# Four graph layers on one core: transposes by VectorE and transfers in place of TensorE, and a planner with other costs

## The chip, the cores and the metric

The kernel runs on one core of a Trainium2 chip. The core has a matrix engine (TensorE, PE in the profile), three engines that work on tiles (VectorE or DVE, ScalarE or ACT, GpSimd or POOL), an engine that issues transfers (SyncE or SP), and 16 DMA engines. The metric is the device time of one execution in microseconds (us), as the median of several runs.

## The reference, cut to what matters

32 graphs, each with 512 nodes of 256 features and its own 512x512 matrix `adj`, go through four layers. Each layer adds a graph network's output to its input and normalizes the rows. All is in 32-bit floats.

```
x = ln(x + relu(((1 + eps)*x + adj @ x) @ W1 + b1) @ W2 + b2)        # layer 0, hidden width 512
x = ln(x + prelu(adj @ (x @ W.T + b)))                               # layer 1
h = ln(x)*gamma + beta                                               # layer 2
x = ln(x + x + relu((adj @ h) @ W_rel + b_rel + h @ W_root))
g = (eps*x + adj @ x) @ W1 + b1                                      # layer 3, hidden width 1024
x = ln(x + silu(g * rsqrt(mean(g*g) + 1e-6) * w) @ W2 + b2)
```

## The kernel before, in words

Each graph is one batch of work. An activation `x` lies in a tile of 128 partitions by 4x256: node `4p + c` is in partition `p`, chunk `c`. All the large products are built as two-by-two block products with seven multiplications in place of eight (`seven`, with block sums made by VectorE in `left_sums` and `right_sums`). `aggregate` makes `adj @ x` in transposed form, features on partitions; `dense_feat` makes the hidden layers with features on partitions; `dense_add` goes back to nodes on partitions and adds onto `x`.

Layer 2 also needs `h` itself with features on partitions. In `layer2` TensorE makes it: 8 transposes of 128x128 (`flip`) into PSUM per batch, then two copies of 128x512. Layer 3 needs the rms scale of each node in every partition, since nodes lie along the columns there: `column_sums` sums over partitions, `inv_sqrt` takes the power on GpSimd, and 4 transposes spread the 512 scales over a PSUM bank `pr`, which VectorE's multiplications then read.

The `1 + eps` of layer 0 and the `eps` of layer 3 are added to the diagonal blocks of `adj` and of two of its block sums (`with_loops`). The four plain blocks are kept in a tile (`kept`, by tile-to-tile transfers, `carry`) and carried back after layer 0 (`restore`). The row vectors `b2` of layers 0 and 3 are added by GpSimd (`plus_row`, four additions of 128x256 each).

The order of all instructions is written out by a planner when the program is built. `Plan.add` records each operation with its possible engines, its cost and its readers and writers. `Plan.order` then places one operation at a time on the engine where it can end first, by a rank that grows with the batch number (`period`) and with the need of TensorE (`needs`); up to `FLIGHT` batches are under way at once. Tiles come from pools (`rooms` of 128x1024, `smalls`, PSUM `banks`), of which a part is held in reserve (`spare`) for older batches. Several rules (`RULES`) are tried, and the one whose plan ends first is taken. The engines then execute the written order, each its own queue in order, and wait on semaphores where operations depend on each other. Transfers are all on SyncE's queue. The planner's costs are fixed numbers: for a transfer, `ISSUE` on the queue, `ADVANCE` until data move, a time by size, and `AFTER` until the reader may start. While `Plan.order` holds a `port` as taken, an operation of VectorE that reads and writes SBUF and one of GpSimd do not overlap.

Of the kernel before, what the change touches and what calls it, by code (L numbers as in the profile page):

```python
# [14 lines left out]
P = 128  # L15
# [11 lines left out]


def in_psum(x):
    return isinstance(x, Part) and x.room.pool.psum  # L30
# [35 lines left out]
def gpsimd_time(n):  # L66
    return 0.15 + n * 0.0024, 0.05


def power_time(n):  # L70
    return 0.37 + n * 0.158, 0.04
# [4 lines left out]
ISSUE, ADVANCE, AFTER, LANES = 0.45, 1.5, 0.35, 8  # L76
# [6 lines left out]
HAND = dict(tensor=0.25, vector=0.13, scalar=0.13, gpsimd=0.18, sync=0.2)  # L83

# [10 lines left out]
RULES = [(50, 2, last, near) for last in (12, 20) for near in (0, 0.5, 1)]  # L95


class Pool:

# [5 lines left out]
    def clear(self):  # L105
        self.rooms = [None] * len(self.tiles)

    def free(self):

        return sorted(  # L110
            (0.0 if r is None else r.until, i)
            for i, r in enumerate(self.rooms)
            if r is None or not r.left
        )


class Room:


    def __init__(self, pool):  # L120
        self.pool = pool
        self.uses = 0
        self.clear()

    def clear(self):
        self.index = None
        self.left = self.uses
        self.until = 0.0


class Part:
# [34 lines left out]
    def place(self):  # L166
        v = self.room.pool.tiles[self.room.index]
        for step in self.steps:
            v = step(v)
        return v  # L170
# [3 lines left out]
class Op:  # L174
# [4 lines left out]
    rank: tuple  # L179
    ways: dict  # L180
    port: set
    yields: bool
    kbytes: float
    rooms: list = field(default_factory=list)
# [6 lines left out]
class Plan:  # L191
# [10 lines left out]
    def grains(self, x):  # L202
        part = isinstance(x, Part)
# [4 lines left out]
        for step, n in dims[:-1]:  # L208
            starts = [s + step * i for s in starts for i in range(n)] if step else starts
        step, n = dims[-1]  # L210
        return {
            (key, g)
            for s in starts
            for g in range(s // grain, (s + step * (n - 1)) // grain + 1)
        }

    def add(self, ways, out, ins, ordered=None, port=(), kbytes=0):
        me = len(self.ops)
        op = Op(self.graph, (self.graph, me), ways, port, "scalar" in ways, kbytes)
        self.ops.append(op)  # L220
        before, results = set(), set()
        writes = self.grains(out) if out is not None else set()
# [22 lines left out]
    def do(self, out, *ways, ordered=None, scrap=None):  # L245
# [3 lines left out]
        port = set()  # L249
        for e, method, _, args, kw in ways:  # L250
            tiles = [x for x in (*args, *kw.values()) if isinstance(x, (bass.AP, Part))]
            ins += tiles
            if e == "gpsimd" and kw.get("op") != ALU.pow or e == "vector" and not (
                method.startswith("bn_") or any(in_psum(x) for x in tiles)
            ):
                port.add(e)
# [19 lines left out]
    def move(self, out, src, kbytes, inward=True):  # L276


        def issue():
            self.nc.sync.dma_start(*(x.place() if isinstance(x, Part) else x for x in (out, src)))  # L280

        self.add(
            {"sync": ((ISSUE, ADVANCE + wire_time(kbytes) + AFTER), issue)},
            out if inward else None, [src] if isinstance(src, Part) else [], kbytes=kbytes,
        )
# [31 lines left out]
    def order(self, period, pace, last, near):  # L317
# [15 lines left out]
        oldest, port, wire, lanes = 0, 0.0, 0.0, [0.0] * LANES  # L333
        can_start = {i for i, n in enumerate(behind) if not n}
        done = []
        while can_start:
# [4 lines left out]
            def rooms_free(op):  # L341

                count = {}
                for r in op.rooms:
                    if r.index is None:
                        count[r.pool] = count.get(r.pool, 0) + 1
                at = 0.0
                for pool, n in count.items():
                    if pool not in room_at:
                        room_at[pool] = pool.free()  # L350
                    n += pool.spare[min(op.graph - oldest, len(pool.spare) - 1)]
                    if op.graph - oldest >= self.flight or n > len(room_at[pool]):
                        return None
                    at = max(at, room_at[pool][n - 1][0])
                return at

            best = {}
            for i in can_start:
# [4 lines left out]
                if op.kbytes:  # L363
                    wait = max(wait, lanes[0])
                at = {
                    e: max(free[e], wait, ready[i][e], port if e in op.port else 0.0)
                    for e in op.ways
                }
                way = min(at, key=lambda e: at[e] + sum(op.ways[e][0]) + (YIELD if op.yields and e == "vector" else 0.0))
# [10 lines left out]
            end = t + busy + tail  # L380
            if op.kbytes:
                wire = max(wire, t + ADVANCE) + wire_time(op.kbytes)
                end = wire + AFTER
                lanes = [*lanes[1:], end]
            if engine in op.port:
                port = end
            for r in op.rooms:
                if r.index is None:
                    r.index = r.pool.free()[0][1]
                    r.pool.rooms[r.index] = r  # L390
# [16 lines left out]
def tile_gnn_stack(ctx: ExitStack, tc: tile.TileContext, a: dict, out: bass.AP):  # L407
# [36 lines left out]
    FLIGHT, ROOMS, SMALL = 4, 36, 12  # L444
# [3 lines left out]
    psum = ctx.enter_context(tc.tile_pool(name="psum", bufs=1, space=bass.MemoryType.PSUM))  # L448
    plan = Plan(nc, FLIGHT)

# [7 lines left out]
    rooms = pool(work, "room", ROOMS, NC * D, P, (0, 4, 6, 8))  # L458
# [5 lines left out]

    def gpsimd(method, n, *args, **kw):
        return "gpsimd", method, gpsimd_time(n), args, kw
# [22 lines left out]
    def both(method, o, x, y, engines):  # L489
        plan.do(o, *(e(method, span(o), x, y) for e in engines))  # L490

    def add(o, x, y, *engines):
        both("tensor_add", o, x, y, engines or (vector,))

    def sub(o, x, y, *engines):
        both("tensor_sub", o, x, y, engines or (vector,))

    def mul(o, x, y):
        both("tensor_mul", o, x, y, (vector,))
# [10 lines left out]
    def carry(o, x):  # L510
        plan.move(o, x, P * span(o) / 256)

    def inv_sqrt(o, x):
        n = span(o)
        plan.do(
            o, ("gpsimd", "tensor_tensor", power_time(n), (x, mhalf[:, 0:n]), dict(op=ALU.pow))
# [3 lines left out]
    def room(*shape):  # L520
        return Part(Room(rooms)).shaped(*shape)

# [57 lines left out]
    nc.vector.memset(mhalf, -0.5)  # L580

# [52 lines left out]
    class Adjacency:  # L634
# [3 lines left out]
        def __init__(self, b):  # L638

            self.halves = [room(HC, N) for _ in range(2)]  # L640
            for m in range(NC):
                chunk = self.halves[m // HC][:, m % HC, :]
                plan.move(chunk, a["adj"][b][:, m, :], P * N / 256)
# [6 lines left out]
        def sums(self):  # L650
# [8 lines left out]
            kept = room(4, HC, P)  # L659
            self.plain = [kept[:, i] for i in range(4)]  # L660
            for d, o in zip(self.plain, self.loops):
                if plan.graph:
                    carry(d, o)
                else:
                    copy(d, o)

        def restore(self):
            for d, o in zip(self.plain, self.loops):
                carry(o, d)

        def with_loops(self, loop):
            for d, o in zip(self.plain, self.loops):
                add(o, d, loop.unsqueeze(1).to_broadcast(list(o.shape)), vector)

        def row_sums(self):

            rows = room(N)
# [79 lines left out]
    def dense_sums(upper, lower):  # L757
# [3 lines left out]
        for pairs in zip(upper, lower):  # L761
            blocks = [x[:, :, j * TH : (j + 1) * TH] for x in pairs for j in range(2)]
            sums = right_sums(*blocks, [room(2, TH) for _ in range(3)], blocks[1])
# [29 lines left out]
    def column_sums(t, put):  # L793
# [3 lines left out]
        few = small(16)  # L797
# [7 lines left out]
        for q in range(1, P // Q):  # L805
            add(few[0:Q], few[0:Q], few[q * Q : (q + 1) * Q])
        for q in range(P // Q):
            put(slice(q * Q, (q + 1) * Q), few[0:Q, q :: P // Q])
# [64 lines left out]

    def plus_row(x, r):

        for c in range(NC):
            add(x[:, c, :], x[:, c, :], r, gpsimd)
# [13 lines left out]
    def load_x(b):  # L891
        x = tok()
        plan.move(x, a["x"][b].rearrange("(p c) d -> p c d", c=NC), N * D / 256)
# [192 lines left out]
```

## Time and profile before

| | before |
|---|---|
| median of 3 runs | 2365.41 us (2363.45 to 2366.38) |
| profiled execution, own time | 2366.02 us |
| its span, first to last instruction | 2364.2 us |
| TensorE busy | 2330.0 us, 14362 matrix instructions |
| VectorE busy | 2138.4 us, 5485 instructions |
| ScalarE busy | 1570.1 us |
| GpSimd busy | 407.7 us |
| granted TensorE clock | 0.997 |
| bytes moved by transfers | 107.25 MB, 45 GB/s on average |

Every 32-bit matrix product appears as two matrix instructions in the profile, a transpose as one. Nearly all instructions carry the same line number, that of the function in which the planner issues them, so groups are told apart by the names of their tiles: `ps` is PSUM, `room` a work tile, `few` a small tile, `L_gnn_W` and `A` weights and sums of weights, `ident` the identity matrix that a transpose uses. The length of an instruction includes the pipeline's depth, so that two neighbours overlap; what one costs in a full queue is the distance between starts.

### The profile page before, as it was taken

How to read it: one execution, taken by the hardware profiler on the slowest of the kernel's cores; microseconds unless marked ns; L12 is line 12 of the kernel's file. 1: busy time of each engine (PE TensorE's matmuls, PEld its weight loads, DVE VectorE, ACT ScalarE, POOL GpSimd, SP SyncE). 2: the span in 40 equal slices, each digit the busy share in tenths (PEclk: the TensorE clock that was granted, in tenths of full speed). 3: DMA queues.
4: the chain of work that ended last, by engine and by line, in shares of the span. 5: the costliest groups of instructions: out<-in, count | busy, mean ns of one | idle time of the engine just before them, and what ended most of it. 6: DMA issues, size and time to landing. Idle time of an engine off the chain costs nothing.

```text
span 2364.2 us, 40948 instructions
## 1 busy us (share of the span) xinstructions
PE 2330.0 (99%) x14362; PEld 2135.4 (90%) x14362; DVE 2138.4 (90%) x5485; ACT 1570.1 (66%) x3994; POOL 407.7 (17%) x422
## 2 busy tenths in 40 slices
PE   8999999999999999999999999999999999989997
PEld 7899989999999999999999999999999989978997
DVE  6899989999999999999999999999999999988997
ACT  3767666667666676766676666776666766565764
POOL 1112111111121121111111211111111112111111
PEclk9999999999999999999999999999999999999999
DMA  7001110111110111101111101111011111011000
GB/s 218 12 8 54 50 54 12 52 50 51 53 35 30 50 54 50 54 14 50 50 52 52 44 20 50 54 50 54 14 50 50 52 52 46 23 52 48 10 10 28
DMA packets 103487, 107.25 MB, mean 45 GB/s; under 512 B 10865, under 2 KB 78193, under 8 KB 103281
## 3 DMA queue, kind: packets, MB, share of 16 engines
q1 hardware_dynamic: 103280, 104.64, 14.5%
q8 instruction: 113, 1.85, 0.3%
q14 instruction: 94, 0.76, 0.1%
HBM read 54.80 MB, written 16.78 MB: 30 GB/s over the span
## 4 chain that ended last, share of the span: by engine, by line
PE 91%; DVE 4%; DMA 2%; ACT 1%; issue 1%; SPq 0%; POOL 0%; POOLq 0%; ACTq 0%; DVEq 0%
PE ps L266 91%; DVE room L266 3%; ACT room L266 1%; DVE few L266 1%; DMA room<-in_x_dram 1%; ACT scrap L266 1%; DMA room<-room 1%; SPq L280 0%; DMA L_gnn_eps<-in_L_gnn_eps_dram 0%; DMA room<-in_adj_dram 0%; POOL few L266 0%; ACT L266 0%; POOLq L1082 0%; DVE L_gnn_W L266 0%; DVE A L266 0%
## 5 line engine op out<-in xcount | busy, mean ns | idle before, releaser
L266 PE MATMUL ps<-room,room 128*128 128x256 f32 x3584 | 911.9, 380 | 9.8 <-DMA room<-in_x_dram 5.8
L266 DVE TENSOR_TENSOR room<-ps,room 128x256 f32<-128x256 f32 (+1 forms) x1344 | 629.6, 475 | 149.3 <-PE ps L266 122.6
L266 PEld LDWEIGHTS ps<-room,room 128*128 128x128 f32 x3584 | 650.1, 191 | 88.8 <-issue 7.1
L266 DVE TENSOR_TENSOR room<-room,room 128x512 f32<-128x512 f32 (+1 forms) x1120 | 640.6, 585 | 9.9 <-ACT room L266 3.1
L266 PE MATMUL ps<-L_gnn_W,room 128*128 128x128 f32 (+1 forms) x3584 | 622.7, 291 | 7.2 <-ACT room L266 4.9
L266 PEld LDWEIGHTS ps<-L_gnn_W,room 128*128 128x128 f32 x3584 | 525.3, 192 | 31.1 <-ACT room L266 7.2
L266 PE MATMUL ps<-A,room 128*128 128x128 f32 x3072 | 489.2, 276 | 1.8 <-ACT room L266 1.1
L266 PEld LDWEIGHTS ps<-A,room 128*128 128x128 f32 x3072 | 434.8, 192 | 15.8 <-ACT room L266 1.3
L266 PE MATMUL ps<-room,L_gnn_W 128*128 128x256 f32 x1536 | 424.6, 380 | 1.0 <-DVE room L266 0.9
L266 ACT ACTIVATE room<-ps,L_gnn_b_c 128x256 f32<-128x256 f32 x768 | 318.2, 472 | 157.2 <-PE ps L266 157.0
L266 POOL TENSOR_TENSOR few<-few,mhalf 128x4 f32<-128x4 f32 (+1 forms) x160 | 212.5, 1329 | 1211.0 <-DVE few L266 1208.5
L266 ACT ACTIVATE room<-ps 128x256 f32<-128x256 f32 (+1 forms) x546 | 215.0, 407 | 298.5 <-PE ps L266 294.7
L266 ACT ACTIVATE room<-room,few 128x256 f32<-128x256 f32 x624 | 341.0, 603 | 107.0 <-DVE few L266 103.7
L266 DVE TENSOR_TENSOR room<-room 128x256 f32<-128x256 f32 (+1 forms) x640 | 330.4, 518 | 18.0 <-DMA room<-in_adj_dram 5.7
L266 POOL TENSOR_TENSOR room<-room,L_gnn_b 128x256 f32<-128x256 f32 x256 | 194.6, 769 | 739.6 <-PE ps L266 519.0
L266 PE MATMUL ps<-room,A 128*128 128x256 f32 x1152 | 319.2, 380 | 3.0 <-ACT room L266 3.0
L266 PEld LDWEIGHTS ps<-room,L_gnn_W 128*128 128x128 f32 x1536 | 279.7, 191 | 33.1 <-DVE room L266 2.2
L266 ACT ACTIVATE room<-room 128x1024 f32<-128x1024 f32 (+2 forms) x260 | 245.8, 946 | 18.1 <-DVE room L266 16.5
L266 ACT ACTIVATE room<-room,L_gnn_rms_weight_c 128x512 f32<-128x512 f32 x256 | 179.7, 718 | 111.3 <-DVE room L266 108.2
L266 PEld LDWEIGHTS ps<-room,A 128*128 128x128 f32 x1152 | 206.5, 191 | 27.1 <-ACT room L266 4.2
L266 ACT ACTIVATE scrap<-room 128x256 f32<-128x256 f32 x384 | 157.2, 411 | 74.3 <-DVE room L266 63.1
L266 ACT ACTIVATE scrap<-room,few 128x256 f32<-128x256 f32 x384 | 190.7, 498 | 18.1 <-DVE few L266 16.3
(53 smaller groups left out, 1453.4 us busy)
## 6 DMA issues: line engine op xcount, KB each, us to landing
room<-in_adj_dram SPq DMA_DIRECT2D x128, 256.0 KB, 5.0
room<-room SPq DMA_DIRECT2D x252, 128.0 KB, 2.2
room<-in_x_dram SPq DMA_DIRECT2D x32, 512.0 KB, 6.0
out_dram<-room SPq DMA_DIRECT2D x32, 512.0 KB, 3.0
L_gnn_W<-in_L_gnn_W_dram SPq DMA_DIRECT2D x2, 1024.0 KB, 8.5
L_gnn_W<-in_L_gnn_W_dram SPq DMA_DIRECT2D x2, 512.0 KB, 8.1
L_gnn_b<-in_L_gnn_b_dram SPq DMA_DIRECT2D x3, 128.0 KB, 5.0
L_gnn_W_rel<-in_L_gnn_W_rel_dram SPq DMA_DIRECT2D x1, 256.0 KB, 7.2
```

Of the source, the lines that this page charges most:

```text
L266: getattr(getattr(self.nc, engine), method)(to, *(put(x) for x in args), **kw)
```

## The change

- **Transposes of h** (`turned`). For all but the first and last batch (`alone`), VectorE transposes 32x32 squares of `h` in two instructions of 128x512, and 16 tile-to-tile transfers of 32 KB carry the squares to their partitions.
- **Scales of layer 3** (`everywhere`). For the same batches, VectorE arranges the scales in a 32x32 square and transposes it; one transfer writes 16x32 numbers to a line in DRAM, a second reads the line into all 128 partitions. The multiplications read this tile where they read PSUM.
- **Diagonals.** From the second batch on, the two blocks of `adj` itself are read again from the input (four transfers of 64 KB), the two of the block sums are stored in DRAM and read back. `with_loops` works in place.
- **Row additions** (`plus_row`) go from GpSimd to VectorE, as two additions of 128x512.
- **Planner.** A tile-to-tile transfer has an issue time of its own, `AFTER` is longer, some loads have an additional `late`, the power costs more, and the power on GpSimd takes part in the port's rule. Dependencies are kept by 32 partitions as well. Tiles can be given out as halves (`short`). Batches in flight are 5 where they were 4, `smalls` 11 where they were 12, the reserves are smaller, and there are three rules with other numbers.

```diff
-ISSUE, ADVANCE, AFTER, LANES = 0.45, 1.5, 0.35, 8
+ISSUE, ADVANCE, AFTER, LANES = dict(sync=0.45, within=0.66, gpsimd=1.5), 1.5, 0.8, 8
...
+TWO_OPERANDS = ("tensor_add", "tensor_sub", "tensor_mul", "scalar_tensor_tensor")
+PORT = 0.25
...
-RULES = [(50, 2, last, near) for last in (12, 20) for near in (0, 0.5, 1)]
+RULES = [(40, 2, 12, 0.25), (40, 2, 20, 0.25), (45, 2.5, 20, 0.25)]
...
-    FLIGHT, ROOMS, SMALL = 4, 36, 12
+    FLIGHT, ROOMS, SMALL = 5, 36, 11
...
-    rooms = pool(work, "room", ROOMS, NC * D, P, (0, 4, 6, 8))
+    rooms = pool(work, "room", ROOMS, NC * D, P, (0, 2, 4, 4))
...
-            kept = room(4, HC, P)
-            self.plain = [kept[:, i] for i in range(4)]
-            for d, o in zip(self.plain, self.loops):
-                if plan.graph:
-                    carry(d, o)
+            if plan.graph:
+                self.kept = next(diagonals)
+                for i in (2, 3):
+                    d = self.kept[:, i - 2]
+                    name = f"{self.kept.tensor.name}{i}"
+                    plan.move(d, self.loops[i], P * HC * P / 256, into=name)
...
         def restore(self):
-            for d, o in zip(self.plain, self.loops):
-                carry(o, d)
+            for i in range(4):
+                if plan.graph == 0:
+                    carry(self.loops[i], self.kept[:, i])
+                elif i < 2:
+                    for k in range(HC):
+                        c = i * HC + k
+                        block = a["adj"][plan.graph][:, c, c * P : (c + 1) * P]
+                        plan.move(self.loops[i][:, k], block, P * P / 256)
+                else:
+                    name = f"{self.kept.tensor.name}{i}"
+                    d = self.kept[:, i - 2]
+                    plan.move(self.loops[i], d, P * HC * P / 256, outof=[name])
...
+    def turned(h):
+
+        hT = Wide(DC)
+        if alone():
+            for k in range(DC):
+                ps = bank(N)
+                for c in range(NC):
+                    flip(ps[:, c * P : (c + 1) * P], h[:, c, k * P : (k + 1) * P])
+                copy(hT.chunk(k), ps)
+        else:
+            squares = Wide(DC)
+            for k in range(DC):
+                o = squares.chunk(k)
+                plan.do(o, vector("transpose", N, h[:, :, k * P : (k + 1) * P]))
+            places = [slice(q * Q, (q + 1) * Q) for q in range(P // Q)]
+            to, of = (
+                x.pair(0).then(lambda v: v.rearrange("p k (c i) -> p (k c) i", i=P))
+                for x in (hT, squares)
+            )
+            for p in places:
+                for q in places:
+                    carry(to[p, :, q], of[q, :, p])
+        return hT
+
+    def everywhere(sums, ops):
+
+        few = small(2, NC)
+        ve, power = few[:, 0, :], few[:, 1, :]
+        by_token(ve, sums, *ops)
+        inv_sqrt(power, ve)
+        if alone():
...
+        else:
+            few = small(2, Q)
+            square, turned = few[0:Q, 0, :], few[0:Q, 1, :]
+            for q in range(P // Q):
+                ts(square[:, q : N // Q : P // Q], power[q * Q : (q + 1) * Q], 1.0, None, ALU.mult)
+            plan.do(turned, vector("transpose", Q, square))
+            o, line = short(N), next(lines)
+            name = line.tensor.name
+            plan.move(line.rearrange("(m i) -> m i", i=Q), turned[0 : N // Q], N / 256, into=name)
+            plan.move(o, line.partition_broadcast(P), P * N / 256, late=0.8, outof=[name])
+        return o
+
     def plus_row(x, r):
 
-        for c in range(NC):
-            add(x[:, c, :], x[:, c, :], r, gpsimd)
+        for h in range(2):
+            add(half(x, h), half(x, h), r.unsqueeze(1).to_broadcast([P, HC, D]))
```

## The prediction

> **What bounds the kernel now.** I read the busy shares first, then the 40 slices, the chain that ended last, the busy time by stretch, and last the timeline of TensorE, for the price of one transpose.
>
> ```profile
> PE 2330.0 (99%) x14362; PEld 2135.4 (90%) x14362; DVE 2138.4 (90%) x5485; ACT 1570.1 (66%) x3994; POOL 407.7 (17%) x422
> ...
> PE   8999999999999999999999999999999999989997
> ...
> PE 91%; DVE 4%; DMA 2%; ACT 1%; issue 1%; SPq 0%; POOL 0%; POOLq 0%; ACTq 0%; DVEq 0%
> ```
>
> TensorE sets the time: it is full in all slices but the first and a few late ones, and the chain lies on it for 91%. VectorE is second with 90%. Busy TensorE is not proof of a full one, since matmuls overlap, so I price it by distances between starts. The timeline of TensorE around one batch's transposes, and the same place a batch later (start, length, instruction; all consecutive rows except where cut):
>
> ```profile
> 990.77 0.49 PE L266 MATMUL ps<-ident,room 128*128 128x128 f32 x3
> 991.10 1.03 PE L266 MATMUL ps<-room,room 128*128 128x256 f32 x4
> 991.96 0.49 PE L266 MATMUL ps<-ident,room 128*128 128x128 f32 x3
> ...
> 995.99 0.60 PE L266 MATMUL ps<-ident,few 128*128 128x128 f32 x4
> 996.42 0.60 PE L266 MATMUL ps<-room,A 128*128 128x256 f32 x2
> ...
> 1062.86 0.49 PE L266 MATMUL ps<-ident,room 128*128 128x128 f32 x3
> ```
>
> Four transposes occupy 996.42 − 995.99 = 0.43 us, 0.108 each; four 128x256 instructions take 991.96 − 991.10 = 0.86, 0.215 each. A batch takes 1062.86 − 990.77 = 72.09 us. The groups give per batch 212 instructions of 128x256, 224 of 128x128 (0.111 each by the same reading) and 12 transposes: 45.6 + 24.9 + 1.3 = 71.8. So in the middle TensorE loses about 0.3 us a batch. Over the whole run 32 × 71.8 = 2298, and 2364.2 − 2298 = 66 is lost, nearly all at the ends. Busy time by stretch (stretch and its length, then busy time and count of PE, PEld, DVE, ACT and POOL, granted clock, DMA share, GB/s):
>
> ```profile
> 0.00:20.00 20.00, 16.81 (x63) 13.77 (x64) 9.97 (x27) 5.59 (x12) 3.57 (x10) 1.00 0.84 273
> 420.00:440.00 20.00, 20.00 (x169) 19.67 (x168) 20.00 (x44) 13.26 (x32) 1.36 (x1) 1.00 0.21 74
> 780.00:800.00 20.00, 20.00 (x168) 19.65 (x167) 20.00 (x43) 13.21 (x31) 0.90 (x1) 1.00 0.22 77
> 800.00:1200.00 400.00, 400.00 (x2459) 367.79 (x2458) 366.14 (x947) 270.81 (x697) 74.09 (x77) 1.00 0.14 42
> 2000.00:2200.00 200.00, 191.60 (x1156) 172.33 (x1155) 169.59 (x440) 122.18 (x326) 33.08 (x36) 1.00 0.16 48
> 2330.00:2364.20 34.20, 21.57 (x168) 20.48 (x167) 24.33 (x70) 11.64 (x20) 4.03 (x4) 0.87 0.12 47
> ```
>
> Two things matter: VectorE is busy 91.5% in the middle, so it has about 6 us a batch to give; and there are 20 us stretches in which VectorE is busy throughout and TensorE still has no hole. A full VectorE does not by itself stop TensorE.
>
> **What the Trainium skill says.** "VectorE: DVE Perf Modes", The three transpose paths: VectorE transposes within 32x32 blocks only. That is why 16 transfers must carry blocks across partitions; no plain VectorE transpose is in this trace. "SBUF — State Buffer", SBUF: two separate sides: VectorE and GpSimd share a pair of ports under an exclusive lock, which matters to VectorE operations with two SBUF inputs. The trace agrees mildly: the 128x256 additions with two SBUF inputs average 447 ns, those that read PSUM 418. "DMA: Bandwidth & Descriptors", Why small descriptors are slow: the penalty concerns HBM and not SBUF to SBUF. The trace has only 512-byte pieces there, so no run so far shows it for 128 bytes.
>
> **The change, part by part.**
>
> *TensorE.* In 30 of 32 batches 8 transposes of h and 4 of the rms scales go: 30 × 12 × 0.108 = 38.9 us. The built order confirms 360 fewer, and every other matmul is unchanged in number. The period should fall to 72.09 − 1.30 = 70.8.
>
> *VectorE*, counted in the built order and priced by start-to-start times (0.60 for 512 columns, 0.33 for 256):
>
> - the row additions: 256 of 128x256 on GpSimd (769 ns each) become 128 of 128x512: +77;
> - 60 transposes of 128x512: the nearest row is the transposing reduction of the same shape, 707 ns long, about 0.6 apart: +36. Bounds: 0.33, the distance of an operation of 256 columns, were it twice as fast; 4 × 311 = 1.24 as an estimate from the skill's figure for 128 columns. That is +20 to +74;
> - 120 more 32x4 operations of 0.16, and 30 small transposes of about 0.1: +22;
> - 44 normalizations that the planner now places there and not on ScalarE: +15; 28 PSUM copies less: −9;
> - less waiting for GpSimd: 448 × 0.03 + 672 × 0.015 = 23 us of excess today; the row additions are half of GpSimd's busy time, so about −11.
>
> Sum +130, so 2138 becomes 2268, and 97% of a span near 2327. Per batch that is 4.3 of the 6 us of room. This is the number on which the forecast hangs. The range of the transpose alone (−16 to +38 in all) moves it between 97 and 99%.
>
> *ScalarE* loses 60 copies of 128x512 and 44 normalizations and gains 28 smaller copies, about 55 us less; at 66% that is worth nothing.
>
> *SyncE and transfers.* Per batch, tile-to-tile transfers of 128 KB (594 ns to issue, 2.2 us to land) fall from 8 to none; 16 of 32 KB in equally many pieces come, with 4 transfers of diagonal blocks to and from DRAM, 4 block loads and 2 for the line of scales. Issue: 8 × 0.59 + 2.5 = 7.3 us before, 20 × 0.59 + 10 × 0.44 + 0.8 = 17 after, of 71. The queue has room. The 16 wait for VectorE's two transposes, take 16 × 0.59 = 9.5 us to issue and land 2.2 later, and behind them stand the output and the next batch's loads, which have tens of us in hand. Five batches in flight cover a chain 12 us longer. I price it at nothing; uncovered, it would be up to 12 us once per batch.
>
> The new line of scales is a store followed by a broadcast load, and VectorE's multiplications queue behind its landing. Nearest rows: 3.0 us for a store, 5.0 for a 128 KB broadcast. The planner counts 2.3 and 3.8 for them. So the line may land up to 1.9 us after the planned moment, or on time, as loads at the start shared a crowded DMA (share 0.84 in the first stretch). I take 0.1 us a batch of cost.
>
> *Planning.* More batches in flight, half rooms and later assumed landings change the order everywhere. The late hole of 8.4 us in the stretch 2000 to 2200 goes with loads that land later (5.0 us) than the old planner's 2.5, so some of it may come back; against it, a tighter VectorE fills ends worse. I take zero for the two.
>
> **Sum.** The profiled execution took 2366.0 with 1.8 around the span. 2366.0 − 38.9 + 3 (line, 30 × 0.1) + 1 (VectorE late now and then) = 2331; the median of the runs stands 0.6 below it: 2330.
>
> **Rivals.**
>
> - *TensorE stays the bound*, as above: 2318 to 2342. For it: the stretches with both full. Chance 0.55.
> - *VectorE becomes the bound together with TensorE.* At 97 to 99% each delay on its queue reaches TensorE. At 0.7 us a batch: 2330 + 21 = 2351, between 2342 and 2360. For it: only 3% left; against it: the same stretches. Chance 0.21.
> - *The ends gain too.* If half of the 57 us lost outside the first 9 us is filled by the fifth batch: near 2302. Little speaks for it, since the loads at the start keep DMA full. Chance 0.05.
> - *Slower: the line lands late.* Place: VectorE's multiplications by the row of scales, once per batch, with the whole of VectorE's queue behind them. Price: 1.9 us by the rows above, 30 × 1.9 = 57, 2387. It decides from (2370 − 2330) / 30 = 1.3 us per batch that nothing absorbs. Against it: that needs the full difference of two rows, and other batches' matmuls to be used up. Chance 0.14.
> - *The gain is lost by a part of this* and ends within 0.2%, 2361 to 2370: 0.05.
>
> **How the numbers follow.** A difference of 0.2% (4.7 us) is about what a measurement here can tell from none. Faster is 0.55 + 0.21 + 0.05 = 0.81, same 0.05, slower 0.14. The likeliest case alone spans 2318 to 2342; the range for 8 in 10 reaches from 2312, leaving out most of the case of the ends, to 2362, taking in VectorE as a second bound and leaving out the late line.
>
> **What would show it.** Right: transposes on TensorE 16 and 8; a period of 70.8 us between equal places; VectorE at 96 to 98%, TensorE at 98 or more; the 32 KB transfers landing near 2.2 us. A VectorE transpose over 0.7 us, or TensorE holes released by VectorE in the middle, would mean the second case. Idle VectorE released by the transfer of the line, 1 us or more per batch, would mean the slower one.

## The result, and the profile after

The changed kernel takes 2349.99 us (median of 4 runs, 2349.04 to 2353.13), the kernel before in the same comparison 2364.88 (4 runs, 2363.45 to 2366.38). The ratio is 0.9939, with a 95% interval from 0.9922 to 0.9957. It is faster by 15 us where 35 were forecast. The profiled execution took 2349.14 us with a span of 2347.2, at a granted clock of 0.999.

The page of the kernel after: the busy shares, the 40 slices of TensorE and VectorE, and the chain that ended last.

```profile
PE 2305.1 (98%) x14002; PEld 2095.8 (89%) x14002; DVE 2209.5 (94%) x5850; ACT 1516.7 (65%) x3918; POOL 233.3 (10%) x166
...
PE   9999999999999999999999999999999999999998
...
DVE  8998999999999999999999999999999999998988
...
PE 84%; DVE 12%; DMA 1%; issue 1%; ACT 1%; SPq 0%; POOLq 0%; DVEq 0%; ACTq 0%
```

The 360 transposes are gone (14362 to 14002), and GpSimd lost nearly half of its time. But the chain lies on TensorE for 84% where it was 91%, and on VectorE for 12% where it was 4%. The slices hide what happened, since 98% and 100% show the same digit. The stretches show it. Busy time by stretch, after (columns as in the prediction):

```profile
400.00:800.00 400.00, 396.39 (x2428) 362.23 (x2427) 379.67 (x1003) 259.71 (x672) 40.34 (x27) 1.00 0.21 55
800.00:1200.00 400.00, 397.01 (x2409) 362.56 (x2408) 379.75 (x1008) 265.35 (x684) 43.43 (x28) 1.00 0.20 51
2000.00:2200.00 200.00, 195.22 (x1135) 174.82 (x1134) 182.69 (x484) 130.47 (x349) 17.09 (x14) 1.00 0.18 44
```

Before, TensorE was busy for 400.00 of 400 us in the middle and VectorE for 366. Now VectorE is at 380, which is 95%, and TensorE has holes, 3 to 3.6 us in 400. The chain shows where they are. A piece of the chain of the kernel after, with start, length and the engine that it lies on:

```profile
427.76 70.31 PE ps L294 x428
498.07 0.02 issue
498.08 1.17 PE ps L294 x8
499.26 0.00 issue
499.26 0.42 DVE room L294
499.68 0.09 DVE few L294
499.77 0.06 issue
499.83 10.26 PE ps L294 x58
```

TensorE runs 70.31 us without a hole. Then come eight matmuls that wait in their queue for nothing, and the next one starts 499.83 − 498.08 = 1.75 us after the first of them, where eight distances of 0.111 would be 0.9: it waits for an addition that reads PSUM and a small operation of VectorE. TensorE's timeline has the same place as an idle time of 0.58 us:

```profile
499.83 1.13 PE L294 MATMUL ps<-A,room 128*128 128x128 f32 x8 [0.58 <-DVE few L294]
```

A batch later the same place comes again: 499.83 − 427.76 = 72.07 us. That was 72.09 before. In the middle of the run the whole saving on TensorE is gone, once per batch, at a wait for VectorE. It is the only hole: between 500 and 1500 us TensorE idles 0.58 us at this place of each batch, 0.02 us just ahead of it, and nowhere else.

The start of each batch's output transfer tells the same and says where the 15 us come from. The times of the 7th, the 25th and the last output:

| | 7th | 7th to 25th | 25th to last |
|---|---|---|---|
| before | 631.8 | 1298.7 | 430.2 |
| after | 691.4 | 1296.0 | 356.0 |

With five batches in flight the first outputs come later and the last ones closer together. The two ends together are 14.6 us shorter, the 18 batches between them 2.7 us. So the gain that was predicted, in the period, did not come, and one that was priced at nothing did.

What the new operations cost, from the groups and the transfers of the kernel after (busy, mean ns; idle before them and its releaser; for transfers size and median us to landing):

```profile
L294 DVE STREAM_TRANSPOSE room<-room 128x512 f32<-128x512 f32 x60 | 38.8, 677 | 0.4 <-ACT room L294 0.3
L294 DVE TENSOR_SCALAR few<-few 32x4 f32<-32x4 f32 x376 | 59.3, 158 | 4.0
L294 PE MATMUL ps<-A,room 128*128 128x128 f32 x3072 | 492.0, 276 | 17.3 <-DVE few L294 13.4 <-DVE room L294 3.5
```

```profile
room<-room SPq DMA_DIRECT2D x480, 32.0 KB, 2.0
room<-line SPq DMA_DIRECT2D x30, 256.0 KB, 3.3
...
line<-few SPq DMA_DIRECT2D x30, 2.0 KB, 1.3
```

None of these is dear: the transposes cost what the forecast took, and the transfers landed early. Yet the matmuls from `A` waited 13.4 us in all for VectorE's small tiles.

**Why VectorE is late.** The planner writes a start for every operation, so the start in the trace can be set against it. How far VectorE is behind the written start, just before four moments of the trace, and its growth per batch between the first and the third (growth, divided by 1000 us, times the period):

```
                 500 us  1000 us  1500 us  2000 us   growth per batch
before             8.28     9.45    10.62    12.36     0.17
after             16.40    26.07    35.37    46.23     1.37
```

This growth is the measured period less the period of the plan. It is therefore nearly the same for TensorE (1.38 in the changed kernel): it says how much a batch loses against its plan, not who loses it. The plan did have the forecast gain in it, 72.1 − 0.2 = 71.9 us a batch before and 72.0 − 1.4 = 70.6 after. The execution did not keep to it.

Who loses it shows within a batch, in steps at the operations on 32 partitions. The timeline of VectorE in the kernel after, up to the hole in TensorE (start, length to the end of the last instruction of the row, instruction):

```profile
478.99 0.42 DVE L294 TENSOR_TENSOR room<-ps,room 128x256 f32<-128x256 f32 x1 [2.36 <-PE ps L294]
...
488.98 0.70 DVE L294 TRANSPOSE_TENSOR_REDUCE few<-room 128x16 f32<-128x512 f32 x1
489.60 0.65 DVE L294 TENSOR_TENSOR room<-room,room 128x512 f32<-128x512 f32 x1
490.28 0.16 DVE L294 TENSOR_TENSOR few<-few 32x16 f32<-32x16 f32 x1
490.48 0.69 DVE L294 TENSOR_TENSOR room<-room 128x512 f32<-128x512 f32 x1
...
493.55 0.67 DVE L294 TENSOR_SCALAR few<-few 32x4 f32<-32x4 f32 x4
494.26 0.76 DVE L294 TENSOR_TENSOR room<-room,loop 128x256 f32<-128x256 f32 x2
...
498.55 0.68 DVE L294 TENSOR_SCALAR few<-few 32x4 f32<-32x4 f32 x4
499.26 0.42 DVE L294 TENSOR_TENSOR room<-ps,room 128x256 f32<-128x256 f32 x1
```

Four operations of 32x4 take 494.26 − 493.55 = 0.71 us, 0.18 each. An addition of 32x16 takes 0.20, and the 128x512 before it 0.68 and not its usual 0.60. The code charges them by `vector_time`, 0.06 + n × 0.00106: 0.064 for 32x4 and 0.077 for 32x16. A batch has 12 of the first (8 before the change; the new four fill the 32x32 square) and 6 of the second: 12 × 0.11 + 6 × 0.2 = 2.5 us, by estimate, that the plan doesn't know of.

From 478.99 to the hole VectorE works without a pause. By 489.60 it has kept the written distances to 0.03 us; at 499.26 it is 1.56 us behind them. Of this, 0.6 us arises at the three additions of 32x16 and their neighbours, 0.44 at the first four 32x4 and 0.45 at the second four; all other operations of the stretch together add less than 0.1. VectorE still idles some 3.6 us a batch, in this one 2.36 of them in the wait for TensorE just ahead of the stretch, but none within it.

The kernel before has 8 × 0.11 + 6 × 0.2 = 2.1 us of the same kind per batch, and lost only 0.17 against its plan. There VectorE has some 6 us of idle time per batch and TensorE no hole.

The Trainium skill describes such an effect: "VectorE: DVE Perf Modes", Two Vector instructions with no wait between them, says that an operation whose input or output begins in another group of 32 partitions than the last one's starts only when all earlier VectorE operations have finished. The section calls this a model and gives no price. The trace agrees in kind: within a run of four 32x4 the starts are 0.17 us apart, about the full length of one (158 ns), and the operation ahead of a 32x16 takes longer.

### The profile page after: what moved, and what is told of

It reads as the page before. It is cut to its first block, busy times and chain, and to the rows that moved or that the text cites. A ratio compares the mean times of both kernels' runs of the same rounds, so it can differ in the third digit from the quotient of the medians.

```text
span 2347.2 us, 40710 instructions
## 1 busy us (share of the span) xinstructions
PE 2305.1 (98%) x14002; PEld 2095.8 (89%) x14002; DVE 2209.5 (94%) x5850; ACT 1516.7 (65%) x3918; POOL 233.3 (10%) x166
## 4 chain that ended last, share of the span: by engine, by line
PE 84%; DVE 12%; DMA 1%; issue 1%; ACT 1%; SPq 0%; POOLq 0%; DVEq 0%; ACTq 0%
PE ps L294 84%; DVE room L294 10%; DVE few L294 2%; ACT room L294 1%; ACT scrap L294 0%; DMA diagonal<-room 0%; SPq L312 0%; DMA L_gnn_eps<-in_L_gnn_eps_dram 0%; DMA room<-in_x_dram 0%; DMA room<-room 0%; DMA room<-in_adj_dram 0%; DVE A L294 0%; POOLq L1194 0%; DVE L_gnn_W L294 0%; DVEq L294 0%
## 5 line engine op out<-in xcount | busy, mean ns | idle before, releaser
L294 PE MATMUL ps<-room,room 128*128 128x256 f32 x3584 | 931.7, 380 | 6.1 <-ACT room L294 2.6
L294 DVE TENSOR_TENSOR room<-room,room 128x512 f32<-128x512 f32 (+1 forms) x1360 | 778.0, 591 | 4.1 <-DMA room<-in_adj_dram 1.7
L294 PEld LDWEIGHTS ps<-room,room 128*128 128x128 f32 x3584 | 613.2, 191 | 62.7 <-ACT room L294 6.5
L294 DVE TENSOR_TENSOR room<-ps,room 128x256 f32<-128x256 f32 (+1 forms) x1344 | 599.1, 471 | 66.9 <-PE ps L294 65.6
L294 PE MATMUL ps<-L_gnn_W,room 128*128 128x128 f32 (+1 forms) x3584 | 583.2, 291 | 4.4 <-DVE room L294 2.2
L294 PEld LDWEIGHTS ps<-A,room 128*128 128x128 f32 x3072 | 466.3, 191 | 68.0 <-issue 17.1
L294 PE MATMUL ps<-A,room 128*128 128x128 f32 x3072 | 492.0, 276 | 17.3 <-DVE few L294 13.4
L294 POOL TENSOR_TENSOR few<-few,mhalf 128x4 f32<-128x4 f32 (+1 forms) x160 | 232.6, 1455 | 2108.2 <-DVE few L294 2084.2
L294 ACT ACTIVATE room<-room,few 128x256 f32<-128x256 f32 x580 | 316.4, 597 | 121.7 <-DVE few L294 121.6
L294 ACT ACTIVATE room<-ps 128x256 f32<-128x256 f32 x514 | 187.9, 376 | 248.4 <-PE ps L294 247.1
L294 DVE TENSOR_TENSOR room<-room 128x256 f32<-128x256 f32 (+1 forms) x640 | 314.3, 496 | 34.4 <-DMA room<-room 13.4
L294 DVE TENSOR_SCALAR few<-few 32x4 f32<-32x4 f32 (+2 forms) x792 | 119.0, 158 | 6.5 <-ACT scrap L294 0.6
```

What stands on the lines that cost most here:

```text
L294: getattr(getattr(self.nc, engine), method)(to, *(put(x) for x in args), **kw)
```

## The experiments

Two theories stood at first. **P**: the planner's price for operations on 32 partitions is wrong, VectorE falls behind the order written for it, and TensorE, whose order has no slack left at that place, waits. **F**: VectorE is simply too full beside a full TensorE.

### Only the prices (e1_price)

```diff
+def moved_time(n):
+    return 0.17 + n * 0.00106, 0.085
+
+def summed_time(n):
+    return 0.25 + n * 0.00106, 0.085
...
-        plan.do(o, vector("tensor_scalar", span(o), x, s1, s2, **kw))
+        times = (vector_time if o.shape[0] == P else moved_time)(span(o))
+        plan.do(o, ("vector", "tensor_scalar", times, (x, s1, s2), kw))
...
-            add(few[0:Q], few[0:Q], few[q * Q : (q + 1) * Q])
+            kw = ("vector", "tensor_add", summed_time(N // Q), (few[0:Q], few[q * Q : (q + 1) * Q]), {})
+            plan.do(few[0:Q], kw)
```

> Only the planner's prices change: a VectorE operation that works on 32 partitions is charged 0.17 us instead of 0.064 (32x4) and 0.27 instead of 0.077 (the 32x16 additions). The same instructions run. Theory P (wrong price): the written order has VectorE late by 1.5 us where TensorE needs it, because these operations take longer than charged; with the right price the period falls from 72.06 us to 70.9 or less and the time to 2312 (2304 to 2322). Theory F (full VectorE): at 95% busy VectorE stops TensorE in any order; the period stays over 71.7 and the time at 2340 or more.

Measured: 2309.51 us (2308.73 to 2310.63), ratio to before 0.9765, interval 0.975 to 0.9779. Outputs come 70.95 us apart on average (9th to 23rd; the single distances alternate between 67 and 75), where the prediction wanted 70.8. The page, then the busy time by stretch, then the chain between 900 and 1300 us, of this kernel:

```profile
PE 2286.4 (99%) x14002; PEld 2095.0 (91%) x14002; DVE 2207.6 (96%) x5861; ACT 1520.1 (66%) x3907; POOL 242.1 (10%) x166
```

```profile
400.00:800.00 400.00, 400.00 (x2481) 368.11 (x2481) 386.56 (x1023) 267.67 (x691) 45.18 (x28) 1.00 0.20 54
800.00:1200.00 400.00, 400.00 (x2452) 367.60 (x2451) 386.31 (x1029) 262.98 (x671) 43.63 (x28) 1.00 0.21 55
```

```profile
899.89 400.19 PE ps L302 x2472
```

TensorE's work is the same; the planner put 11 more operations on VectorE and as many fewer on ScalarE. VectorE is fuller in the middle than in the changed kernel (386 of 400 us, not 380), and TensorE has no hole. Theory F falls. A batch loses 0.32 us against its plan in place of 1.37.

The other prices give another order, so a luckier order is a rival. The plans themselves decide: as the kernels write them out, the last operation starts at 2287.9 us in the changed kernel and at 2288.3 here. This order is no shorter than the other; it is the one that the execution keeps to. This version beats both kernels, by 40 us the changed one.

### The uncharged operations doubled (e2_twice)

```diff
-    def do(self, out, *ways, ordered=None, scrap=None):
+    def do(self, out, *ways, ordered=None, scrap=None, twice=False):
...
-            getattr(getattr(self.nc, engine), method)(to, *(put(x) for x in args), **kw)
+            for _ in range(2 if twice else 1):
+                getattr(getattr(self.nc, engine), method)(to, *(put(x) for x in args), **kw)
...
+                plan.do(o, vector("tensor_scalar", span(o), x, 1.0, None, op0=ALU.mult), twice=True)
```

> The change, with each of the four 32x4 operations per batch that lay out the scales for the small transpose issued twice (the second writes the same values); the planner does not know, so the order is otherwise that of the change. It adds 4 x 0.17 = 0.68 us of uncharged VectorE time per batch just ahead of the place where TensorE waits. Theory P: nothing absorbs it, the period rises by 0.5 to 0.7 us to 72.6 to 72.75, the time by 15 to 21 us to 2365 to 2371. Theory F: VectorE has 3.6 us idle per batch and only its total counts; the period rises by less than 0.2 us, the time by less than 6.

Measured: 2374.07 us (2372.39 to 2378.12), ratio 1.0045 (1.003 to 1.006), 24 us more than the change, somewhat over what was expected. The spacing of the outputs is 72.78 us, 0.76 more, which is 0.19 for each of the four added operations. VectorE's timeline and TensorE's, at the same place of the batch as above:

```profile
501.65 1.45 DVE L295 TENSOR_SCALAR few<-few 32x4 f32<-32x4 f32 x8
```

```profile
503.70 1.13 PE L295 MATMUL ps<-A,room 128*128 128x128 f32 x8 [1.36 <-DVE few L295]
```

TensorE's hole grew from 0.58 to 1.36 us. At this place of the changed kernel the time of a 32x4 operation reaches TensorE whole: nothing absorbs it.

### Which price, and whether it must be on those operations

The first kernel (e10_moved) keeps only `moved_time`, the second (e11_summed) only `summed_time`. The third (e12_spread) leaves both at the wrong value and charges other operations more:

```diff
 def vector_time(n):
-    return 0.06 + n * 0.00106, 0.085
+    return (0.08 if n >= 256 else 0.06) + n * 0.00106, 0.085
```

> Of the two prices corrected in e1_price only the first: VectorE operations with two scalars on 32 partitions (12 a batch) are planned with 0.17 us, the additions of 32x16 stay at 0.077. Theory P (VectorE becomes late where the plan counts too little for just these operations): 12 x 0.11 = 1.3 of the 1.55 us of lateness per batch goes, so most of the gain of e1_price is there: 2308 to 2325, period 70.9 to 71.3. Theory S (any planned slack on VectorE would do, and both prices add up): about half of the gain, 2325 to 2335.

> Only the second price: the six additions of 32x16 a batch are planned with 0.27 us, the small operations with two scalars stay at 0.064. Theory P: 1.3 us of lateness per batch remains uncounted, but a part of the gain comes, 2325 to 2345, period 71.3 to 71.9; if the additions were the whole cause, 2308 to 2318.

> The small operations keep the prices of the change; instead each VectorE operation of 256 columns and more that is planned by the plain formula costs 0.02 us more in the plan (about 100 a batch, so some 2 us a batch, as much as e1_price adds in all). Theory P (the price has to be on the operation that is late): the lateness arises as before where the small operations stand together, 2335 to 2352, period over 71.5. Theory S (any slack of that size takes the lateness up before it reaches TensorE): 2306 to 2320, period near 70.95.

| kernel | us (range) | ratio to before | last start in the plan, us | loss per batch against the plan, us |
|---|---|---|---|---|
| change | 2349.99 (2349.04 to 2353.13) | 0.9939 (0.9922 to 0.9957) | 2287.9 | 1.37 |
| only 32x16 priced | 2347.63 (2346.54 to 2348.05) | 0.9919 (0.9905 to 0.9934) | 2294.8 | 1.28 |
| other operations dearer | 2341.22 (2340.0 to 2343.62) | 0.9894 (0.988 to 0.9909) | 2299.1 | 0.92 |
| only 32x4 priced | 2331.40 (2330.49 to 2332.66) | 0.9851 (0.9835 to 0.9868) | 2288.8 | 0.95 |
| both priced | 2309.51 (2308.73 to 2310.63) | 0.9765 (0.975 to 0.9779) | 2288.3 | 0.32 |

The 32x4 price alone brings 19 of the 40 us: 6 us less gain than theory P required, and in the range that was given to the rival S. The 32x16 price alone brings 2, outside its range and not told from none by the intervals; its plan is 7 us longer. Together they bring 40, so they do not add up as S would have it: while either is wrong, a batch still loses about 1 us. Slack put elsewhere brings 9 us, inside the range of P and 21 us short of S. But the last two columns say that P is not the whole truth either: this slack takes the loss down to 0.92, as far as the 32x4 price does, and pays for it with a plan that is 11 us longer. So slack anywhere takes up a part. Only both prices, on the operations themselves, take up most of the loss, and they do not lengthen the plan. The chain of the kernel with only the 32x4 price, between 900 and 1300 us, shows what is left:

```profile
by line: PE ps L302 81.8%; DVE room L302 15.3%; DVE few L302 1.8%; issue 1.1%; DVEq L302 0.1%
```

VectorE still holds 17% of it.

### The prices in the kernel before (e7_before_price)

The same two prices, in the kernel before the change.

> The kernel before with the two corrected prices and nothing else. Theory P: there TensorE is already full (400.00 of 400 us in the middle) and VectorE has 8% idle, which takes the uncounted 2 us a batch up; so correct prices have nothing to win, 2358 to 2372, period 72.0 to 72.3, and the gain of e1_price belongs to the change. Rival: the prices alone are worth some tens of us whatever the rest of the kernel, 2325 to 2345.

Measured: 2403.19 us (2399.77 to 2408.57), ratio 1.0168 (1.0151 to 1.0185): both expectations missed, and in the direction that neither had. A batch loses 0.2 us against its plan there, no more than before. It is the order itself that is worse: the last operation of the plan starts at 2380.1 us where it was 2343.9, which is 36 of the 38 us. A piece of its chain:

```profile
977.45 2.69 ACT room L274 x6
...
981.02 5.24 DMA room<-in_adj_dram
986.36 1.30 DVE room L274 x2
...
990.25 21.98 PE ps L274 x108
1012.33 8.43 DVE room L274 x18
```

TensorE's work comes to stand behind a load of `adj` and a row of VectorE's sums. The planner places one operation at a time, so a truer price can lead to a worse order. That limits what the first experiment shows: not that right prices help a kernel, but that in the changed one the uncounted time was the loss. The result does exclude that the prices are worth 40 us whatever the rest of the kernel.

### The transposes back on TensorE, with the prices right (e8_price_flips)

```diff
     def alone():
 
-        return plan.graph in (0, B - 1)
+        return True
```

> The run with the right price (2309.5), with the 12 transposes per batch back on TensorE and the transfers for them gone. Both theories: TensorE has 30 x 1.30 = 39 us more; if TensorE is the bound there as its profile says, period 72.1 to 72.4 and time 2342 to 2356. A smaller difference to 2309.5 would mean that VectorE and not TensorE bounds that kernel.

Measured: 2361.97 us (2361.11 to 2363.22), ratio 0.9987 (0.998 to 0.9994), 6 us above the upper end of the expected range. Busy time in the middle:

```profile
800.00:1200.00 400.00, 400.00 (x2470) 366.95 (x2468) 375.13 (x970) 268.56 (x690) 34.60 (x27) 1.00 0.12 38
```

TensorE is full again, the outputs are 72.28 us apart, and VectorE has 25 us in 400 to spare. Against the version with both prices this is the transposes alone, under equal rules and prices, apart from the order that the planner then writes: 2361.97 − 2309.51 = 52 us, of which 30 × (72.28 − 70.95) = 40 is in the period. The other 12 were not followed up. The prediction said 38.9. The step for TensorE was right; in the change its gain was there and was lost again.

### Relief for VectorE: row additions back on GpSimd

```diff
-        for h in range(2):
-            add(half(x, h), half(x, h), r.unsqueeze(1).to_broadcast([P, HC, D]))
+        for c in range(NC):
+            plan.do(x[:, c, :], ("gpsimd", "tensor_add", (0.15 + D * 0.0024, 0.05), (x[:, c, :], r), {}))
```

This was run in the change, and in the change with `alone` always true (all transposes on TensorE).

> The change, with the row additions on GpSimd as before (four of 128x256, 0.77 us each for the planner). VectorE is relieved by 2.4 us per batch, the small operations stay wrongly charged. Theory F: with VectorE at 92% TensorE is full again, period 70.7 to 71.0, time 2310 to 2320. Theory P: the lateness of up to 1.5 us is absorbed only where the new order leaves VectorE idle before TensorE needs it; the period lands between 70.8 and 71.8, the time between 2315 and 2345, with TensorE's holes behind the small operations.

> The new planner, diagonals and half rooms with the old operations: all batches transpose on TensorE and GpSimd adds the rows (0.77 us an operation for the planner). TensorE has its 1.30 us per batch back, VectorE loses about 4 us per batch. Theory P and F alike: period 72.0 to 72.2, no holes on TensorE in the middle. If the 15 us of the change came from the ends by the planner alone, the time is 2345 to 2355; if they came from the removed transposes, 2360 to 2368.

Measured: 2460.81 us (ratio 1.0405) and 2416.52 us (1.0216), both far above every expectation. The timelines of VectorE and of GpSimd in the first of them:

```profile
1002.86 1.21 DVE L294 SCALAR_TENSOR_TENSOR room<-room,nalpha,room 128x512 f32<-128x512 f32 x1
1004.00 0.94 DVE L294 TENSOR_TENSOR room<-room,room 128x256 f32<-128x256 f32 x1
1004.86 0.86 DVE L294 SCALAR_TENSOR_TENSOR room<-L_gnn_b,few,ps 128x256 f32<-128x256 f32 x2
...
1006.85 0.74 DVE L294 SCALAR_TENSOR_TENSOR room<-room,nalpha,room 128x512 f32<-128x512 f32 x1
1007.51 0.15 DVE L294 TENSOR_SCALAR few<-few 128x2 f32<-128x2 f32 x1
```

```profile
1002.75 1.91 POOL L294 TENSOR_TENSOR room<-room,L_gnn_b 128x256 f32<-128x256 f32 x2 [3.86 <-DVE room L294]
```

The same operation takes 1004.00 − 1002.86 = 1.14 us while GpSimd adds, and 0.66 when it does not; the addition after it takes 1004.86 − 1004.00 = 0.86, where one of that shape just ahead took 0.33. The planner of the change frees the port after `PORT` = 0.25 us of a GpSimd operation, since it now thinks of the power. So these two kernels measure another uncharged cost of the same kind. They were run again with the port held for the whole addition:

```diff
-                port["vector"] = t + PORT
+                port["vector"] = t + (PORT if op.kbytes == 0 and busy > 1.0 else busy)
```

> The change with the row additions on GpSimd, the planner keeping VectorE off for the whole of each; the small operations stay wrongly charged. Theory F (full VectorE): VectorE is relieved, TensorE is full, period 70.6 to 71.0, time 2305 to 2318. Theory P (wrong price): the lateness of 1.5 us per batch is still there and is absorbed in part, period 70.9 to 71.9, time 2315 to 2345.

> As the run with the old operations and the new planner, but the planner now keeps VectorE off for the whole 0.77 us of a row addition on GpSimd and not for 0.25 us. If the loss of that run (period 74.3 us, 2416) came from VectorE standing behind GpSimd's row additions at moments that the planner counts as free, the period falls to 72.0 to 72.3. Then the time tells where the 15 us of the change came from: 2343 to 2355 if from the planner's work on the start and the end, 2360 to 2368 if from the removed transposes.

Measured: 2365.36 us (2363.13 to 2368.48; ratio 1.0, 0.9991 to 1.0008) and 2378.51 us (2377.72 to 2379.72; 1.0053, 1.0038 to 1.0068). Holding the port is worth 95 and 38 us. Both still lie above what was expected, so where the 15 us of the change came from isn't settled by this pair. In the first, VectorE is busy for 376 of 400 us in the middle and TensorE for 397. VectorE is no fuller than in the changed kernel (380), and a batch loses more against its plan, 1.71 us. The 32-partition prices are still wrong here; how the loss divides between them and additions that still collide was not tried.

### The narrow operations kept within one group of 32 partitions (e9_same_rows)

The 32x4 operations read and write partitions 0 to 31 only. This kernel so leaves out the spreading of layer 1's row sums and of layer 3's mean squares over the other 96 partitions (in layer 3 a constant 1 stands there).

```diff
-            ts(o[q * Q : (q + 1) * Q], sums[:, q :: P // Q], *ops)
+            ts(o[0:Q], sums[:, q :: P // Q], *ops)
...
-                ts(square[:, q : N // Q : P // Q], power[q * Q : (q + 1) * Q], 1.0, None, ALU.mult)
+                ts(square[:, q : N // Q : P // Q], power[0:Q], 1.0, None, ALU.mult)
```

> The change with its wrong prices; each 32x4 operation now reads and writes partitions 0 to 31, where the change reads or writes the four groups of 32 partitions in turn. So the sums and scales do not reach their partitions (their place is left out; the constant 1 stands there). Same count and size of operations. If moving between groups of partitions is what makes them slow, their distance falls from 0.17 to 0.07 us, the period from 72.06 to 70.8 to 71.4, the time to 2308 to 2328. If narrow operations are slow in themselves, the distance stays at 0.17, the period at 72 and the time at 2345 to 2352.

Measured: 2355.30 us (2354.24 to 2356.49), ratio 0.9956: neither range. As a test of the time it is inconclusive: the loss per batch stayed at 1.34, since eight of the twelve operations did not become shorter. The four that fill the square did. VectorE's timeline:

```profile
501.15 0.36 DVE L294 TENSOR_SCALAR few<-few 32x4 f32<-32x4 f32 x4
501.44 0.67 DVE L294 SCALAR_TENSOR_TENSOR room<-room,room 128x512 f32<-128x512 f32 x1
```

Four take 501.44 − 501.15 = 0.29 us, 0.07 each, as the planner believed. So the narrow shape isn't what is dear. The other eight write the same places one after the other in this kernel and stayed 0.17 to 0.19 apart (two single distances were over 0.2). The semaphores in the trace tell them apart: each of these waits for VectorE's own semaphore, that is for an operation ahead of it on the same engine, and neither the four nor the runs of four in the changed kernel do so within a run. Without such a wait, all 276 distances within runs of four in the changed kernel are between 0.153 and 0.177 us, and all 82 in this kernel, where the partitions stay the same, between 0.066 and 0.079. What is dear is the move between groups of partitions.

## Why the prediction was right or wrong

**TensorE, −38.9 us.** Right in mechanism and size: 360 transposes went, and under equal prices they are worth 40 us in the period. It isn't visible in the result because the period is set by the wait for VectorE.

**The step that failed** is the cost of VectorE's lateness, "+1 (VectorE late now and then)", with the reading behind it, "A full VectorE does not by itself stop TensorE". The sentence is true (the version with both prices has VectorE at 97% beside a full TensorE) but it was the wrong question. VectorE does not stop TensorE by being full. It stops it where its real times are longer than the written order assumes and the order leaves it no idle time before TensorE needs the result. The 6 us a batch of room were an average over the batch; in the 20 us ahead of the hole there was none. The prediction counted the added 32x4 operations at a real 0.16 us, and never set that beside the 0.064 that the planner charges for them. Over the 30 batches the term was not 1 us but about 30 × (72.07 − 70.95) = 34, an estimate from the two periods; the two kernels differ by 40.

**VectorE's busy time** was forecast at 2268 us and 97%, and is 2209.5 and 94%. The row additions (87, forecast 77), transposes (38.8, forecast 36), the small operations (24, forecast 22) and normalizations (16, forecast 15) were priced nearly right. Two terms were not. The other two-input operations of 128x512 on work tiles, with the 240 multiplications that came in among them from PSUM, fell by 25 us together, which the forecast did not have. And groups whose count did not change lost about 57 us of busy time, where the forecast had 11 for the relief from GpSimd. Mean lengths times counts account for 30 of the 57; the rest is closer overlap of neighbours. That GpSimd is the cause was not tried. The forecast's own figure for it was a choice of lines: of three groups of 128x256 additions with two inputs in SBUF it took the one with 447 ns on average, while the other two had 419 and 416, as short as those that read PSUM (418). The error was on the cautious side, and the second rival came about all the same.

**ScalarE, SyncE and the transfers, nothing.** Right. The 32 KB transfers landed in 2.0 us (forecast 2.2). VectorE waited 13.4 us in all, in 16 waits, for transfers from tile to tile, and TensorE has no hole behind these waits in the middle.

**The line of scales, 0.1 us a batch.** Cheaper still: 1.3 us for the store and 3.3 for the load in place of 3.0 and 5.0 in the nearest rows, both below what the planner counts. No wait of VectorE for the line shows in the trace, so the slower rival is refuted.

**Planning, zero.** Wrong in size: the ends gained 15 us. The third rival, that the ends gain too, came about with half the gain that it named, and hid how complete the loss in the middle was. In the run with all transposes on TensorE and both prices, outputs are 72.28 us apart where they were 72.10 before, and yet it takes 3.7 us less than the kernel before: by estimate 3.7 + 30 × 0.18 = 9 us at the ends belong to the planner and not to the transposes. Whether the fifth batch in flight did it, as the rival said, or another change of the planner was not tried.

**The rivals.** The second, VectorE as a second bound at 2351 us with 0.7 us lost per batch, hits the time to 1 us. It did so by two errors that cancel: the loss was 1.1 us per batch, and the ends gave 15 us back. Its own sign, holes of TensorE released by VectorE in the middle, was named and is there; its stated reason, that VectorE is 97% full, isn't the cause. The closeness of its number is luck.

## What to carry to other kernels

Where the order of instructions is written out beforehand, lay the charged cost of each kind of operation beside its measured distance between starts, above all for small operations that a change adds. Idle time can hide wrong costs, and a change that takes it away lets them show. Count uncharged time against the room that is left ahead of the place where the bounding engine waits, not against the average over a batch. And a truer cost is no gain in itself, since a planner that places one operation at a time may answer it with a worse order: run it.

## What the runs showed of the hardware

- A VectorE operation of 32x4 that moves between groups of 32 partitions takes 0.17 to 0.18 us from start to start, within one group 0.07, unless it waits for VectorE's own semaphore (then 0.17 to 0.19). An addition of 32x16 takes 0.1 to 0.2 us, depending on what follows, and the operation ahead of it about 0.1 more than it would.
- In the stretch shown, GpSimd additions of 128x256 delay two VectorE operations with two inputs in SBUF by 0.5 us each (0.66 to 1.14, and 0.33 to 0.86). The prediction had read this lock from mean durations as a mild one; a mean over all operations of a shape does not show it.
- A VectorE transpose of 128x512 in 32x32 squares takes 677 ns, hardly different from an addition of that shape (678). One square of 32x32 takes 192 ns.
- The power on GpSimd of 128x8 took 2671 ns on average in the changed kernel, 1672 before, and 1760 in the version with both prices. What lengthens it was not tried.
